# Layer 1's attention: the multiply by the reciprocal sums moved from chunk 1 to chunk 2, with a buffer of its own for the reciprocals

## The chip, the core and the metric

The kernel runs on one core of a Trainium2 chip. The core has a matrix engine (PE in the profile; its weight loads are listed apart as PEld), a vector engine (VectorE, DVE), a scalar engine (ScalarE, ACT), a general engine (GpSimd, POOL) and a queue engine that starts transfers (SyncE, SP). Each works through its own list of instructions; semaphores make one wait for another. Working memory is SBUF, and the matrix engine writes into PSUM. The metric is the device time of one execution in microseconds (us), the median of several runs.

## What is computed

Two layers, each a cross attention and a feed-forward network, over 8 batches of 112 tokens of width 512, with a context of 375 rows for each batch. The change lies in layer 1's attention. Cut to that part, the reference is:

```
q, k, v = proj(hs, Wq, bq), proj(at, Wk, bk), proj(at, Wv, bv)      # 16 heads of 32
scores = clip(einsum('bhsd,bhtd->bhst', q, k) / sqrt(32), -50, 50)
scores = clip(where(attend, scores, -10000.0), -50, 50)
probs  = softmax(scores, axis=-1)
ctx    = einsum('bhst,bhtd->bhsd', probs, v)                        # heads' outputs
delta  = rs * (ctx @ Wo.T + bo)
delta  = layernorm(delta) * gamma + beta
x      = x + delta
```

After it comes layer 1's feed-forward network with 8-bit weights, `down(silu(gate) * up)`, which takes the layer-normed x.

## The kernel before, in words

The softmax is taken without dividing first. For each batch the kernel forms e = exp(score), sums e times v into `num` and e alone into `den`, and multiplies `num` by the reciprocal of `den` at the end.

A loop runs over 8 batches b and, inside, over 3 chunks c of 125 context rows. In this stage the order on every engine is the order in which the program writes the instructions; it was laid out by hand. Each step (b, c) does:

- `scores(b, c)` (L894): 16 small matmuls (L900; 32 in the trace, two passes each) write the scores of the 16 heads into four PSUM tiles, one for each row group r. VectorE clips each of the four into an SBUF tile (L905), and ACT takes the exponential in place (L906). There are exactly four such PSUM tiles, so the scores of the next chunk can't begin before the clips of this one have read theirs.
- The SBUF tiles for e are three sets of four (`sets`). Chunk (b, c) uses set (b + c) modulo 3.
- `fill(1)`: one piece of the key and value projections of a later batch (L193 or L202) on the matrix engine. `STEPS` leaves it out in chunk 2 of batch 4.
- `sums` (L911): the matmuls of e with v (L926) for the chunk before. For the last chunk of a batch, which is summed in chunk 0 of the next batch, `den` too (L921). Its second operand is chunk 0's and 1's e added beforehand, `added`, by `add` (L892): on GpSimd for batches 0 to 6, on VectorE for batch 7. Then ACT copies `den` into `rden` (L932) and `num` into the columns b*112 to (b+1)*112 of `qT` (L933), where the queries of that batch were.
- Chunk 1: `divide(b - 1)` (L936) on VectorE: a reciprocal in place (L937) and a multiply of those columns of `qT` (L939).
- Chunk 2, from batch 2 on: `project_product(b - 2)`, the output projection of the tile of 128 tokens with that number. It reads columns (b-2)*128 to (b-1)*128 of `qT` (L798). `project_begin` (L804 and on) adds the bias and begins the layer norm on VectorE and GpSimd.
- Chunk 0, from batch 3 on: `project_end(b - 3)` (L817 and on) ends it and takes the moments of the next layer norm. `write4` and `transpose4` (L832, L839, L842, L843) prepare that tile for the feed-forward network; the transpose follows the projection on the matrix engine.

The weights of the feed-forward network are loaded and converted alongside (L864, L875, L877). After the loop the last batch is summed and divided, and the feed-forward network runs (L1026, L1044), beginning with two blocks of its gate and up products, then the last tile's projection.

Before the change, `rden` is `added[0]`: the first tile of the set that held the added e, free once the `den` matmuls have read it. The next to write it are the clips of chunk 2 of the following batch.

Of the kernel before, what the change touches and what calls it, by code (L numbers as in the profile page):

```python
# [23 lines left out]
F32 = mybir.dt.float32  # L24
# [11 lines left out]
P = 128  # L36
B, T, D = 8, 112, 512
KC = D // P
# [32 lines left out]
def two_layers(ctx: ExitStack, tc: tile.TileContext, x, ctxT, ctxN, mask0, mask1, w1, w2, w3,  # L71
# [10 lines left out]
    def slab(name, dtype=F32):  # L82
        return slabs.tile([P, SLAB], dtype, name=name, tag="slab")
# [126 lines left out]
    def fill(n=1):  # L210
        for _ in range(n):
            next(kv_steps, None)
# [602 lines left out]
    def project_end(i):  # L815
        d, f = updates.pop(i)
        nc.vector.scalar_tensor_tensor(xs[i], d, f, xs[i], ALU.mult, ALU.add)  # L817
        bn = stat.tile([P, nc.vector.BN_STATS_DIM], F32, name="bn", bufs=4)
        nc.vector.bn_stats(bn, xs[i])
        nc.vector.bn_aggr(mv4[:, i, :], bn)  # L820
        var = stat.tile([P, 1], F32, name="ln4_var")
        nc.vector.tensor_scalar_add(var, mv4[:, i, 1:2], LN_EPS)
        rsqrt_pool(var, rstd4[:, i:i + 1], "ln4")
# [22 lines left out]
    with tc.tile_pool(name="work2", bufs=1, side="right") as work2, \  # L846
            tc.tile_pool(name="ps_av", bufs=1, space=PSUM) as ps_av, \
            tc.manual_schedule(engines={ENGINES.PE, ENGINES.SP, ENGINES.DVE,
                                        ENGINES.Activation, ENGINES.Pool}):

        todo = [(w, which, half, c, min(PIECE, HALVES[which][half + 1] - c))
                for which, w in enumerate((wg, wu, wd)) for half in range(2)
                for c in range(HALVES[which][half], HALVES[which][half + 1], PIECE)]
        due = {(0, 1): 2, (0, 2): 2, (1, 0): 1, (1, 1): 2, (1, 2): 2, (2, 0): 1,
               (3, 1): 2, (3, 2): 2, (4, 0): 1, (5, 1): 2, (5, 2): 2, (6, 0): 1,
               (6, 1): 2, (6, 2): 2, (7, 0): 1, (7, 1): 2, (7, 2): 2}
        loaded = []

        def load_integers(count):
            for w, which, half, c, n in todo[:count]:
                raw = work2.tile([P, PIECE], I32, name="raw", bufs=2)[:, :n]
                nc.sync.dma_start(out=raw, in_=w[:, c:c + n])  # L864
                loaded.append((raw, which, half, c - HALVES[which][half], n))
            del todo[:count]

        def convert_integers():
            for raw, which, half, c, n in loaded:
                if (which, half) not in halves:  # L870
                    halves[which, half] = slab("w", F32R)
                t = halves[which, half][:, c:c + n]

                k = pieces.pop()
                nc.scalar.activation(t, raw, AF.Square, bias=zero_point,  # L875
                                     accum_out=squares[:, k:k + 1])
                nc.gpsimd.tensor_scalar(t, raw, -128.0, 1.0, ALU.add, ALU.mult)  # L877
            loaded.clear()

        sets = [[work2.tile([P, KC, T], F32, name=f"e{i}{r}") for r in range(NR)]
                for i in range(NCK)]

        def add(b):
            add = (nc.gpsimd if b in ADD_POOL else nc.vector).tensor_add
            for r in range(NR):  # L890
                e, e1 = (sets[(b + c) % NCK][r][:CK] for c in range(2))
                add(e, e, e1)  # L892

        def scores(b, c):  # L894
            kT = kvs_of[b][0]
            ss = [ps_s.tile([CK, KC, T], F32, name="s") for r in range(NR)]
            for dc in range(KC):
                for r in range(NR):
                    rows = slice(r * HD, (r + 1) * HD)
                    nc.tensor.matmul(ss[r][:, dc, :], lhsT=kT[rows, dc, c * CK:(c + 1) * CK],  # L900
                                     rhs=qT[rows, dc, b * T:(b + 1) * T], start=True, stop=True)
            es = sets[(b + c) % NCK]
            for r in range(NR):
                e = es[r][:CK]
                nc.vector.tensor_scalar(e, ss[r], upper[:, c, b:b + 1], -CLIP, ALU.min, ALU.max)  # L905
                nc.scalar.activation(e, e, AF.Exp, scale=SC1)  # L906
            return es

        def sums(b, c, es):  # L911
            if c == 0:
                sums.num = ps_av.tile([P, KC, T], F32, name="num")
            num = sums.num
            v = kvs_of[b][1]
            if c == NCK - 1:
                den = ps_av.tile([P, KC, T], F32, name="den")
                added = sets[b % NCK]
                for k, of in enumerate((added, es)):
                    for r in range(NR):  # L920
                        nc.tensor.matmul(den[r * HD:(r + 1) * HD], lhsT=ones[:CK, :HD],  # L921
                                         rhs=of[r][:CK], start=(k == 0), stop=(k == 1))
            for dc in range(KC):
                for r in range(NR):
                    head = slice((4 * dc + r) * HD, (4 * dc + r + 1) * HD)
                    nc.tensor.matmul(num[r * HD:(r + 1) * HD, dc, :], lhsT=v[:, c, head],  # L926
                                     rhs=es[r][:CK, dc, :], start=(c == 0 and dc == 0),
                                     stop=(c == NCK - 1 and dc == KC - 1))
            if c == NCK - 1:

                rden = added[0]
                nc.scalar.copy(rden, den)  # L932
                nc.scalar.copy(qT[:, :, b * T:(b + 1) * T], num)  # L933
                rdens[b] = rden

        def divide(b):  # L936
            nc.vector.reciprocal(rdens[b], rdens[b])  # L937
            cols = slice(b * T, (b + 1) * T)
            nc.vector.tensor_mul(qT[:, :, cols], qT[:, :, cols], rdens[b])  # L939


        STEPS = [3, 3, 3, 3, 2, 3, 3, 3]
        ADD_POOL = range(B - 1)
        last, rdens, later = None, {}, []
        counts = list(due.values())
        load_integers(counts.pop(0))
        for b in range(B):
            for c in range(NCK):
                if c == 2 and b in ADD_POOL:
                    add(b)  # L950
                if (b, c) in due:
                    convert_integers()
                    if counts:
                        load_integers(counts.pop(0))
                es = scores(b, c)
                if c == 2 and b not in ADD_POOL:
                    add(b)
                if c < STEPS[b]:
                    fill(1)
                if c == NCK - 1:  # L960
                    sums(*last)
                if (b, c) == (B - 1, NCK - 1):
                    over = tailp.tile([P, 29], F32, name="over")
                    nc.gpsimd.tensor_scalar(over, squares, WIDE, 1.0, ALU.is_gt, ALU.mult)
                if c == 0:
                    while later:
                        later.pop()()
                    if b >= 3:
                        project_end(b - 3)
                elif c == 1 and b >= 1:  # L970
                    divide(b - 1)
                elif c == 2:
                    turned = 3 <= b < 3 + GROUPS[0][1]
                    if turned:
                        write4(b - 3)
                    if b >= 2:
                        project_product(b - 2)
                    if b == B - 1:

                        hits = ps_s.tile([1, 29], F32, name="s")  # L980
                        nc.tensor.matmul(hits, lhsT=ones[:, :1], rhs=over, start=True, stop=True)
                        wide = tailp.tile([1, 1], I32, name="wide")
                        nc.vector.tensor_reduce(wide, hits, AX.X, ALU.max)
                    if b >= 2:
                        project_begin(b - 2)
                    if turned:
                        later.append(transpose4(b - 3, ps_mm, "mm"))
                if last and c < NCK - 1:
                    sums(*last)
                last = b, c, es  # L990

        nc.scalar.activation(stat.tile([CK, 1], F32, name="peak")[:], es[-1][:CK, 0, :1], AF.Silu)
        sums(*last)
        divide(B - 1)
        project_end(B - 3)
    kvs.close()

# [180 lines left out]
```

## Time and profile before

| | us |
|---|---|
| median of 3 runs | 523.79 (523.18 to 524.82) |
| the profiled execution | 523.3 |
| its span, first to last instruction | 521.4 |
| matmuls of scores, L900, whole kernel | 28.9 busy, 768 matmuls |
| clips, L905, whole kernel | 58.9 busy, 96 of 0.677 |
| reciprocals, L937, 8 of them | 2.94 each |
| multiplies, L939, 8 of them | 0.625 to 1.579, median 1.082 |
| add on GpSimd, L892, for one batch | 4.4 to 4.9 |

A row of an engine's timeline gives start, duration, engine, line, operation and tiles; "x4" means that four like instructions are merged into one row. A bracket at the end tells how long the engine stood idle before it, and what ended that. A row of the list of waits gives who waited for whom, the total, the number of times and the longest. Matmuls are pipelined: a group of them that lasts longer than its like has been held up inside, and the profile then counts the hold as busy.

### The profile page before, as it was taken

How to read it: one execution, taken by the hardware profiler on the slowest of the kernel's cores; microseconds unless marked ns; L12 is line 12 of the kernel's file. 1: busy time of each engine (PE TensorE's matmuls, PEld its weight loads, DVE VectorE, ACT ScalarE, POOL GpSimd, SP SyncE). 2: the span in 40 equal slices, each digit the busy share in tenths (PEclk: the TensorE clock that was granted, in tenths of full speed). 3: DMA queues.
4: the chain of work that ended last, by engine and by line, in shares of the span. 5: the costliest groups of instructions: out<-in, count | busy, mean ns of one | idle time of the engine just before them, and what ended most of it. 6: DMA issues, size and time to landing. Idle time of an engine off the chain costs nothing.

```text
span 521.4 us, 8802 instructions
## 1 busy us (share of the span) xinstructions
PE 504.7 (97%) x3380; PEld 317.0 (61%) x3380; DVE 335.7 (64%) x801; ACT 252.6 (48%) x438; POOL 134.8 (26%) x222
## 2 busy tenths in 40 slices
PE   9999999999999998889999999999999999999995
PEld 6445554454554455578655555555555788889983
DVE  3552548767788987784465588997897774434432
ACT  0336746857655656033876266466665224103310
POOL 0000211111011272020542376576762440000000
PEclk9999999999999999898999999999999999999998
DMA  8998795200210100041152111011321000010001
GB/s 232 334 411 345 252 350 189 70 2 0 87 54 1 60 2 0 2 143 52 52 170 64 60 49 44 23 51 38 86 63 52 22 1 1 16 46 20 1 20 45
DMA packets 13231, 45.75 MB, mean 88 GB/s; under 512 B 1969, under 2 KB 3008, under 8 KB 12032
## 3 DMA queue, kind: packets, MB, share of 16 engines
q1 hardware_dynamic: 11744, 41.43, 23.3%
q0 software_dynamic: 1280, 3.70, 2.1%
q8 instruction: 28, 0.46, 0.4%
q14 instruction: 19, 0.16, 0.1%
q10 hardware_dynamic: 160, 0.01, 0.0%
HBM read 41.46 MB, written 1.84 MB: 83 GB/s over the span
## 4 chain that ended last, share of the span: by engine, by line
PE 79%; DVE 12%; POOL 2%; ACT 2%; DMA 2%; issue 2%; DVEq 0%; ACTq 0%; POOLq 0%
PE mm L202 14%; PE s L1026 14%; PE mm L193 12%; PE down L1044 7%; PE mm L539 5%; PE mm L429 4%; PE mm L798 4%; PE s L400 4%; PE s L900 4%; PE num L926 3%; PE den L921 2%; PE mm L579 2%; DVE e L905 2%; DVE e L937 1%; DMA rs<-in_rscale_dram 1%
## 5 line engine op out<-in xcount | busy, mean ns | idle before, releaser
L202 PE MATMUL mm<-wv,cT 128*125 128x512 f32 x192 | 88.7, 606 | 0.0
L193 PE MATMUL mm<-cT,wk 128*128 128x375 f32 x256 | 87.4, 486 | 0.0
L1026 PE MATMUL s<-h4T,w 128*128 128x512 f32 (+1 forms) x352 | 72.6, 367 | 0.2 <-PE num L926 0.2
L905 DVE TENSOR_SCALAR e<-s,upper 125x448 f32<-125x448 f32 x96 | 58.9, 677 | 18.5 <-PE s L900 17.7
L1026 PEld LDWEIGHTS s<-h4T,w 128*128 128x128 f32 x352 | 63.6, 188 | 8.8 <-issue 0.5
L906 ACT ACTIVATE e<-e 125x448 f32<-125x448 f32 x96 | 51.8, 571 | 28.1 <-DVE e L905 27.5
L193 PEld LDWEIGHTS mm<-cT,wk 128*128 128x128 f32 x256 | 46.8, 190 | 27.6 <-issue 0.9
L202 PEld LDWEIGHTS mm<-wv,cT 128*125 128x125 f32 x192 | 35.0, 190 | 38.8 <-issue 37.2
L892 POOL TENSOR_TENSOR e<-e,e 125x448 f32<-125x448 f32 x28 | 33.3, 1221 | 14.6 <-PE num L926 14.6
L1044 PE MATMUL down<-w,gu 128*128 128x512 f32 x154 | 36.4, 393 | 0.0
L539 PE MATMUL mm<-w_q,q_qT 128*128 128x512 fp8e4 (+1 forms) x168 | 34.6, 361 | 1.6 <-ACT q_qT L351 1.1
L437 POOL DMA_DIRECT2D tokens<-x x14 | 10.7, 768 | 90.4 <-DVE x L431 62.7
L1034 ACT CAST gu<-gu 128x512 fp32r<-128x512 f32 (+1 forms) x22 | 12.5, 568 | 41.5 <-DVE gu L1032 41.5
L875 ACT ACTIVATE w<-raw,zero_point 128x640 fp32r<-128x640 int32 (+2 forms) x29 | 22.6, 782 | 20.1 <-DMA raw<-in_wd_dram 9.1
L1044 PEld LDWEIGHTS down<-w,gu 128*128 128x128 f32 x154 | 28.7, 188 | 6.1
L568 POOL TENSOR_SCALAR q<-gu 128x704 bf16<-128x704 f32 x14 | 10.8, 790 | 79.9 <-ACT gu L565 79.9
L877 POOL TENSOR_SCALAR w<-raw 128x640 fp32r<-128x640 int32 (+2 forms) x29 | 20.8, 727 | 38.7 <-DVE e L905 25.3
L900 PE MATMUL s<-qT,kv 32*125 32x112 f32 x768 | 28.9, 280 | 0.3
L539 PEld LDWEIGHTS <-q_qT 128*128 128x128 bf16 x168 | 16.3, 98 | 20.4 <-issue 1.9
L1032 DVE SCALAR_TENSOR_TENSOR gu<-s,su,gu 128x512 f32<-128x512 f32 (+1 forms) x22 | 15.0, 684 | 20.8 <-PE s L1026 19.2
L900 PEld LDWEIGHTS s<-qT,kv 32*125 32x125 f32 x768 | 24.2, 183 | 6.5 <-issue 4.9
L798 PE MATMUL mm<-wo,qT 128*128 128x512 f32 x56 | 25.8, 603 | 1.0 <-DVE qT L939 1.0
(237 smaller groups left out, 794.5 us busy)
## 6 DMA issues: line engine op xcount, KB each, us to landing
cT<-in_ctxT_dram SPq DMA_DIRECT2D x13, 750.0 KB, 6.0
raw<-in_w_dram SPq DMA_DIRECT2D x6, 1408.0 KB, 22.3
cN<-in_ctxN_dram SPq DMA_DIRECT2D x8, 768.0 KB, 5.7
raw<-in_wg_dram SPq DMA_DIRECT2D x8, 320.0 KB, 3.0
raw<-in_wu_dram SPq DMA_DIRECT2D x8, 320.0 KB, 2.9
raw<-in_wd_dram SPq DMA_DIRECT2D x8, 320.0 KB, 3.1
out_dram<-d SPq DMA_DIRECT2D x7, 256.0 KB, 2.0
wk<-in_wk_dram SPq DMA_DIRECT2D x4, 256.0 KB, 5.1
```

Source lines behind the costliest of these rows:

```text
L193: nc.tensor.matmul(ps[dc], lhsT=wk_s[:, kc, dc * P:(dc + 1) * P], rhs=cT[:, kc, :], start=(kc == 0), stop=(kc == KC - 1))
L202: nc.tensor.matmul(ps, lhsT=cT[:, kc, c * CK:(c + 1) * CK], rhs=wv_s[:, kc, :], start=(kc == 0), stop=(kc == KC - 1))
L400: nc.tensor.matmul(s, lhsT=hT0[b][:, kc, :], rhs=cTs[b][:, kc, :], start=(kc == 0), stop=False)
L539: nc.tensor.matmul(ps[:, :n], lhsT=qT[:, kc, :], rhs=w[:, kc * H + n0:kc * H + n0 + n], start=(kc == 0), stop=(kc == KC - 1))
L798: nc.tensor.matmul(ps, lhsT=qT[:, kc, i * P:(i + 1) * P], rhs=wo_s[:, kc, :], start=(kc == 0), stop=(kc == KC - 1))
L875: nc.scalar.activation(t, raw, AF.Square, bias=zero_point, accum_out=squares[:, k:k + 1])
L892: add(e, e, e1)
L900: nc.tensor.matmul(ss[r][:, dc, :], lhsT=kT[rows, dc, c * CK:(c + 1) * CK], rhs=qT[rows, dc, b * T:(b + 1) * T], start=True, stop=True)
L905: nc.vector.tensor_scalar(e, ss[r], upper[:, c, b:b + 1], -CLIP, ALU.min, ALU.max)
L906: nc.scalar.activation(e, e, AF.Exp, scale=SC1)
L1026: nc.tensor.matmul(ps[:, :n], lhsT=w[:, c:c + P], rhs=h4T[k][:, kc, :n], start=(kc == 0 and k == 0), stop=(kc == KC - 1 and k == 1))
L1044: nc.tensor.matmul(ps, lhsT=gus[k][:, hc, j * P:(j + 1) * P], rhs=w[:, c:c + D], start=(hc == 0 and k == 0), stop=(hc == HC - 1 and k == 1))
```

## The change

The reciprocals get a tile of their own in the stage's pool, `rden`, in place of `added[0]`. `divide` is split in two: `invert`, the reciprocal, stays in chunk 1; `scale`, the multiply, goes to chunk 2, behind that chunk's scores and clips (and in batch 7 behind the add on VectorE), ahead of `write4` and of the projection. After the loop both stand one after the other, as before.

```diff
-                rden = added[0]
+                rden = work2.tile([P, KC, T], F32, name="rden")
                 nc.scalar.copy(rden, den)
                 nc.scalar.copy(qT[:, :, b * T:(b + 1) * T], num)
                 rdens[b] = rden
 
-        def divide(b):
+        def invert(b):
             nc.vector.reciprocal(rdens[b], rdens[b])
+
+        def scale(b):
             cols = slice(b * T, (b + 1) * T)
             nc.vector.tensor_mul(qT[:, :, cols], qT[:, :, cols], rdens[b])
...
                 elif c == 1 and b >= 1:
-                    divide(b - 1)
+                    invert(b - 1)
                 elif c == 2:
+                    if b >= 1:
+                        scale(b - 1)
                     turned = 3 <= b < 3 + GROUPS[0][1]
                     if turned:
                         write4(b - 3)
...
         sums(*last)
-        divide(B - 1)
+        invert(B - 1)
+        scale(B - 1)
         project_end(B - 3)
```

## The prediction, made before the changed kernel was run

> **What bounds the kernel now.** I read the busy shares first, then what the matrix engine waited for, then its order of instructions beside VectorE's in the stage that the diff touches (the attention of layer 1, 244 to 403 us).
>
> ```profile
> PE 504.7 (97%) x3380; PEld 317.0 (61%) x3380; DVE 335.7 (64%) x801; ACT 252.6 (48%) x438; POOL 134.8 (26%) x222
> ...
> PE mm L798 <- DVE qT L939: 1.0, 1, 1.0
> ...
> 274.64 1.96 PE L900 MATMUL s<-qT,kv 32*125 32x112 f32 x32
> ...
> 308.31 1.79 PE L900 MATMUL s<-qT,kv 32*125 32x112 f32 x32
> ...
> 312.75 0.97 PE L926 MATMUL num<-e,kv 125*32 125x112 f32 x32
> 313.65 3.70 PE L798 MATMUL mm<-wo,qT 128*128 128x512 f32 x8
> ...
> 329.52 1.14 PE L900 MATMUL s<-qT,kv 32*125 32x112 f32 x32
> 330.60 0.97 PE L926 MATMUL num<-e,kv 125*32 125x112 f32 x32
> 332.56 3.70 PE L798 MATMUL mm<-wo,qT 128*128 128x512 f32 x8 [0.99 <-DVE qT L939]
> ...
> 308.84 2.94 DVE L937 RECIPROCAL e<-e 128x448 f32<-128x448 f32 x1
> 311.88 1.20 DVE L939 TENSOR_TENSOR qT<-qT,e 128x448 f32<-128x448 f32 x1
> 313.20 2.46 DVE L905 TENSOR_SCALAR e<-s,upper 125x448 f32<-125x448 f32 x4
> ...
> 328.84 2.94 DVE L937 RECIPROCAL e<-e 128x448 f32<-128x448 f32 x1
> 331.88 0.62 DVE L939 TENSOR_TENSOR qT<-qT,e 128x448 f32<-128x448 f32 x1
> 332.62 2.46 DVE L905 TENSOR_SCALAR e<-s,upper 125x448 f32<-125x448 f32 x4
> ```
>
> The matrix engine is busy 97% of the span. From here to the end nothing else sets the time for long, so each microsecond that it waits in this stage is a microsecond at the end, and a gain can only come from its waits. There are few. A group of score matmuls (L900) takes 1.14 us unhindered; at 274.64 it took 1.96 and at 308.31 it took 1.79, because its four PSUM tiles were still being clipped (L905): 0.82 and 0.65 us. A third at 369.00 took 1.48 (0.34). The projection (L798) waited 0.99 us for the multiply (L939) in batch 4, and a transpose waited 0.28 us for an ACT copy in batch 6. These five, 3.1 us, are the most that any faster order on VectorE could win here.
>
> The second thing to see is the order reciprocal (2.94 us), multiply (0.62 to 1.58 us), four clips (2.46 us), and how close the projection follows: in batch 3 the multiply ends at 313.08 and the projection starts at 313.65; in batch 4 it was already late.
>
> **What the Trainium skill says.** "TensorE: Matmul & The Clock Gate", section Architectural detail, says that VectorE takes its instructions strictly in order and that the matrix engine pulls only weight loads ahead, its matmuls staying in order. The trace agrees: every clip group and every L798 stands where the program puts it. "SBUF — State Buffer", section Who interferes with whom, says that a VectorE instruction with two SBUF inputs contends with a GpSimd instruction that reads SBUF. The trace agrees on the whole: the multiply took 0.63 us in batch 7 with GpSimd idle, and 1.20, 1.58 and 1.24 us beside GpSimd's adds (L892) in batches 3, 5 and 6. Of the clock gate the first page says (Part 1) that the array's clock halves after about one idle window of 3.4 us; no idle stretch of this stage is that long (granted clock 1.00 throughout), so nothing here shows it.
>
> **The change, part by part.**
>
> *The place.* The ACT copy of the sums (L932, 0.53 us) writes another buffer of the same shape; the reciprocal and multiply read it. No instruction is added. Its one buffer is rewritten in chunk 0 of the next batch, after the previous multiply, so nothing waits. In the tail ACT's first Silu (L1031) waits 4.65 us for L939, probably because its buffer lies over the old place; the matrix engine waits only 0.21 us around there, so releasing it is worth nothing. Cost 0.
>
> *The multiply behind the clips.* The clips of chunk 2 start about 1.1 us earlier (multiply 1.04 us, the mean of its eight, and two gaps). Who gains: the score matmuls of the next batch, if they wait on these clips. That is so once, at 274.64 (batch 2, chunk 0): its clips end at 275.43 and would end near 274.3, so 0.82 us goes. At 308.31 and 369.00 the matmuls wait for the clips of chunk 1, late through the layer norm of a previous tile, which the change doesn't move. From batch 2 on, the projection lies between chunk 2's clips and the next scores, so nothing is left to win.
>
> Who loses: project_product(b-2), in the same chunk 2, reads columns (b-2)*128 to (b-1)*128 of qT, and the multiply of batch b-1 writes (b-1)*112 to b*112. These overlap for every b from 2 to 7. So the projection still needs the multiply, which now stands behind four clips. With E the end of the reciprocal, the multiply is done at E + 2.46 + 1.04 = E + 3.5. The matrix engine's readiness is read from the trace. Its shift and VectorE's are the same from batch to batch, because VectorE's next work (L804) starts at the end of each projection.
>
> - b=2: E 289.11, done 292.6; projection ready 293.8. No wait, 1.2 us to spare.
> - b=3: E 311.78, done 315.28; ready 313.72. Wait 1.56.
> - b=4: E 331.78, done 335.28; it started at 332.56 before. 2.72 more than the old 0.99, 3.7 in all (scores and sums of this chunk have no key/value work between, STEPS[4] is 2).
> - b=5: E 350.56, done 354.06; ready 354.11. Nothing.
> - b=6: E 372.17, done 375.67; ready 374.11. Wait 1.56; the transpose's old wait of 0.28 behind it goes: 1.28.
> - b=7: here VectorE also does the add (L892, 2.23 us) between clips and multiply. E 392.38, done 398.11; ready 396.99. Wait 1.12, and VectorE now lags by the 0.28 that the matrix engine got back: 1.40.
> - b=8, after the loop: the same order as before, 0. project(6) finds the multiply done 2.9 us before it asks (408.11 against 410.97).
>
> Sum: -0.82 + 1.56 + 2.72 + 0 + 1.28 + 1.40 = +6.1 us. Behind the waiting projection stand the transpose and the next scores on the matrix engine, and L804 with a whole layer norm on VectorE and GpSimd; all move along, and after 403 us the matrix engine has no slack that would take a delay up.
>
> The profiled execution took 523.3 us (span 521.4 and 1.9 around it): 529.4. The median of the runs, 523.79, lies 0.49 above it: 529.9.
>
> **Bounds.** Unseen is what the multiply costs in its new position. All at 0.62: waits 1.14, 2.30, 0, 0.86 and 0.98, less 0.82: +4.5. All at 1.58: 2.10, 3.26, 0.49, 1.82 and 1.94, less 0.82: +8.8. I take the mean of the eight, since GpSimd's adds and conversions reach over the new position in batches 3, 5 and 6, and are nearly over in batch 4. So 528.3 to 532.6 for this mechanism. The wait in batch 4 is near the clock window's length; one such window at half speed would be an estimate of 1.7 us from that page, and below nothing it can't go.
>
> **The rivals.**
>
> 1. As forecast: the multiply becomes the last to arrive at the projection. For it: the dependency by columns and the traced times. 529.9, chance 0.72.
>
> 2. The other side, not slower: the multiply stays hidden, and only the earlier clips count. Place: the score groups of the next batch, price 0.82 us, up to the five waits' 3.1 us if the earlier clips also speed the exponentials and PSUM copies behind them. It decides from the point where the projection gets ready later than E + 3.5 us (E + 5.7 in batch 7). For it: batches 2 and 5 meet this, the latter by 0.05 us. Against: batches 3, 4, 6 and 7 miss it by 1.1 us or more. 523.0, at best 520.7; chance 0.09, of which 0.05 within what counts as no change.
>
> 3. Only part of it bites: VectorE gets through its chain sooner than I add up, and only batches 4 and 7 wait: -0.8 + 2.3 + 1.0 = +2.5, 526.3. For it: batches 3 and 6 depend on when GpSimd's port comes free. Against: even the fast multiply leaves about 1 us there. Chance 0.08.
>
> 4. More: every multiply slow (+8.8), and a clock window lost (1.7): 532.6 to 534.3. For it: GpSimd's busy stretches and the long gap of batch 4. Chance 0.09.
>
> 5. The change doesn't do what it says, the multiply landing where it was: 523.8. Against: VectorE's order is the program's. Chance 0.02.
>
> **How the numbers follow.** The measurement tells about 0.3% (1.6 us) from no change. Slower: rivals 1, 3 and 4, 0.89. No change: 0.05 of rival 2 and rival 5, 0.07. Faster: the rest of rival 2, 0.04. The range is 1's bounds, drawn down to take in half or more of rival 3 and up a little into rival 4: 526.6 to 532.9.
>
> **What would show it.** In the new profile: L798 waiting for the multiply four times, some 1.6, 3.7, 1.6 and 1.4 us in batches 3, 4, 6 and 7, none in 2; no score group of 1.96 us in batch 2, chunk 0; clips starting directly after each reciprocal; VectorE's busy time the same within 3 us (only the port's share of the multiply can change); the stage from 403 us on as long as before, only later. I am wrong if L798 doesn't wait on VectorE, or if waits appear in the tail instead.

## The result, and the profile after

The changed kernel takes 531.37 us (median of 4 runs, 530.74 to 532.34) where the kernel before takes 523.54 in the same comparison: a ratio of 1.0147, 95% interval 1.0123 to 1.017, 7.8 us slower. The profiled execution has a span of 529.6 us against 521.4; of that difference of 8.2 us, 8.1 lie between batch 1's first scores and the feed-forward network (152.30 us against 144.21; called the stage below).

The busy shares, the list of what the matrix engine waited for, and the rows of its output projection (L798) and of VectorE's reciprocal, clips and multiply (now L941) answer to the lines shown of the kernel before:

```profile
PE 505.2 (95%) x3380; PEld 316.4 (60%) x3380; DVE 337.0 (64%) x801; ACT 252.3 (48%) x438; POOL 132.8 (25%) x222
```

```profile
PE mm L798 <- DVE qT L941: 6.5, 3, 3.1
...
PE mm L798 <- ACT w L875: 2.2, 2, 1.7
```

```profile
274.13 1.14 PE L900 MATMUL s<-qT,kv 32*125 32x112 f32 x32
...
292.44 3.70 PE L798 MATMUL mm<-wo,qT 128*128 128x512 f32 x8
...
314.06 3.67 PE L798 MATMUL mm<-wo,qT 128*128 128x512 f32 x8 [1.69 <-DVE qT L941]
...
335.06 5.25 PE L798 MATMUL mm<-wo,qT 128*128 128x512 f32 x8 [3.10 <-DVE qT L941]
...
358.62 3.67 PE L798 MATMUL mm<-wo,qT 128*128 128x512 f32 x8 [0.47 <-ACT w L875]
...
380.36 3.67 PE L798 MATMUL mm<-wo,qT 128*128 128x512 f32 x8 [1.72 <-ACT w L875]
...
404.50 3.70 PE L798 MATMUL mm<-wo,qT 128*128 128x512 f32 x8 [1.72 <-DVE qT L941]
```

```profile
307.49 2.94 DVE L937 RECIPROCAL rden<-rden 128x448 f32<-128x448 f32 x1
310.35 2.36 DVE L905 TENSOR_SCALAR e<-s,upper 125x448 f32<-125x448 f32 x4
312.63 1.29 DVE L941 TENSOR_TENSOR qT<-qT,rden 128x448 f32<-128x448 f32 x1
...
334.34 0.66 DVE L941 TENSOR_TENSOR qT<-qT,rden 128x448 f32<-128x448 f32 x1
...
400.84 3.05 DVE L892 TENSOR_TENSOR e<-e,e 125x448 f32<-125x448 f32 x4
403.82 0.62 DVE L941 TENSOR_TENSOR qT<-qT,rden 128x448 f32<-128x448 f32 x1
```

Three things are to be seen. The busy times are the same as before within 2 us; what was added is waiting. The projection waits in five of its six calls in the loop, and each time starts just after the multiply's end: 312.63 + 1.29 is 313.92, and it starts at 314.06; in batch 4, 334.34 + 0.66 is 335.00, and it starts at 335.06. (Two of the waits are put down to ACT's conversion L875, which ended a little later than the multiply; an experiment below shows that they are the multiply's.) And in batch 4 the projection itself lasts 5.25 us, not 3.70. The granted clock in short stretches there (start and end, length, then busy time by engine; the third number from the end is the clock of the matrix engine) tells why:

```profile
329.00:332.00 3.00, 2.95 (x97) 2.43 (x96) 3.00 (x2) 1.35 (x3) 2.21 (x4) 1.00 0.03 5
332.00:335.00 3.00, 0.00 (x0) 0.00 (x0) 3.00 (x7) 2.28 (x4) 2.52 (x3) 0.96 0.01 3
335.00:337.00 2.00, 1.94 (x3) 0.91 (x4) 0.46 (x2) 0.03 (x1) 0.00 (x0) 0.50 0.00 0
337.00:339.00 2.00, 2.00 (x5) 0.94 (x4) 0.00 (x0) 0.00 (x0) 0.00 (x0) 0.70 0.00 0
```

While the matrix engine idled for 3.1 us its clock fell to half, and it stayed there for about 3.2 us of the projection (0.50 over two, and 0.70 over the next two). Half of that, 1.6 us, is what the projection lost: 5.25 against 3.70.

The starts of the projections, after minus before, give the account. They are -1.33, +0.41, +2.50, +4.58, +6.32 and +7.58 us for batches 2 to 7, and +7.58 for the feed-forward network. Read as differences:

| Place | forecast, us | measured, us |
|---|---|---|
| before batch 1's sums | 0 | -0.51 |
| scores of batch 2, chunk 0 (1.96 to 1.14) | -0.82 | -0.82 |
| wait, batch 3 | +1.56 | +1.74 |
| wait, batch 4 (beyond the old 0.99) | +2.72 | +2.09 |
| batch 4's projection at half clock | 0 | +1.54 |
| wait, batch 5 | 0 | +0.54 |
| wait, batch 6, less the transpose's old wait | +1.28 | +1.24 |
| wait, batch 7 | +1.40 | +1.79 |
| feed-forward network | 0 | +0.62 |
| sum | +6.1 | +8.2 |

The first and the last measured rows lie in parts that the change doesn't touch: differences between two executions. The part from the feed-forward network on took 118.2 to 119.1 us over all the profiles of this study, with no order by kernel.

### The profile page after: what moved, and what is told of

The parts are those of the page before. It is cut to its first block, busy times and chain, and to the rows that moved or that the text cites. A ratio compares the mean times of both kernels' runs of the same rounds, so it can differ in the third digit from the quotient of the medians.

```text
span 529.6 us, 8788 instructions
## 1 busy us (share of the span) xinstructions
PE 505.2 (95%) x3380; PEld 316.4 (60%) x3380; DVE 337.0 (64%) x801; ACT 252.3 (48%) x438; POOL 132.8 (25%) x222
## 4 chain that ended last, share of the span: by engine, by line
PE 73%; DVE 14%; DMA 3%; POOL 3%; ACT 3%; issue 2%; SPq 0%; ACTq 0%; POOLq 0%; DVEq 0%
PE s L1031 14%; PE mm L193 12%; PE mm L202 11%; PE down L1049 7%; PE mm L798 5%; PE mm L539 5%; PE mm L429 4%; PE s L400 4%; PE s L900 2%; DVE e L905 2%; PE num L926 2%; PE mm L579 2%; DVE rden L937 2%; PE den L921 2%; DMA rs<-in_rscale_dram 1%
## 5 line engine op out<-in xcount | busy, mean ns | idle before, releaser
L905 DVE TENSOR_SCALAR e<-s,upper 125x448 f32<-125x448 f32 x96 | 58.5, 671 | 17.5 <-PE s L900 17.5
L798 PE MATMUL mm<-wo,qT 128*128 128x512 f32 x56 | 27.3, 632 | 8.7 <-DVE qT L941 6.5
L892 POOL TENSOR_TENSOR e<-e,e 125x448 f32<-125x448 f32 x28 | 30.9, 1137 | 13.9 <-PE num L926 13.9
L875 ACT ACTIVATE w<-raw,zero_point 128x640 fp32r<-128x640 int32 (+2 forms) x29 | 22.6, 780 | 22.1 <-DMA raw<-in_wd_dram 9.4
```

The lines of the kernel that those rows point to most:

```text
L798: nc.tensor.matmul(ps, lhsT=qT[:, kc, i * P:(i + 1) * P], rhs=wo_s[:, kc, :], start=(kc == 0), stop=(kc == KC - 1))
L875: nc.scalar.activation(t, raw, AF.Square, bias=zero_point, accum_out=squares[:, k:k + 1])
```

## The experiments

The theory: the projection reads columns of `qT` that the multiply writes, so it waits for whatever stands before the multiply on VectorE; the wait is the loss, and where it is long the clock can fall too. Rivals: the new buffer costs something, VectorE is late for other work, or the slow projection has a cause of its own. Times are to be read against the kernel before on the same chip: its median was 524.68 us beside the place alone, the dependency taken away, batch 4 alone and the work in batch 4's gap; 522.97 beside batch 1 alone, the add moved and the split; 523.85 beside the repeat, the first try in all four gaps and the split with `write4` ahead; 523.45 beside the second try and GpSimd taken out. Differences in us are differences of these medians, unless a ratio is said. The stage's time is that of the profiled execution.

**The place alone.** The multiply is moved back to chunk 1; `rden` stays in its own tile.

```diff
+        LATE = ()
...
                     invert(b - 1)
+                    if b not in LATE:
+                        scale(b - 1)
                 elif c == 2:
-                    if b >= 1:
+                    if b in LATE:
                         scale(b - 1)
```

> The reciprocals' own tile alone; the multiply stays in chunk 1. Theory (the projection waits for the late multiply): 0 against the kernel before, 523.2 to 523.9 us, the score group in chunk 0 of batch 2 stalls again by 0.8 us, the projection of batch 4 waits 1.0 us. Rival (the new place costs or gives something, through waits on its single buffer or the room below it): a difference of over 1 us.

Measured: 524.48 us, ratio 0.9999 (0.9983 to 1.0015). In the trace the score group of batch 2 took 1.76 us again and batch 4's projection waited 0.97 us. The place is worth nothing that can be told (within 0.9 us), and the rival falls.

**The dependency taken away.**

```diff
-            nc.vector.tensor_mul(qT[:, :, cols], qT[:, :, cols], rdens[b])
+            divided = work2.tile([P, KC, T], F32, name="divided")
+            nc.vector.tensor_mul(divided, qT[:, :, cols], rdens[b])
```

> The changed kernel, with every multiply of chunk 2 written to a tile of its own, so that the projection reads the heads' outputs undivided: the division is left out of what is computed, all instructions remain. Theory (the whole loss is the projection waiting for the multiply, with its clock): the waits in batches 3, 4, 6 and 7 vanish, the gain of 0.8 us in batch 2 stays, and the wait of 1.0 in batch 4 goes too: 521.5 to 523 us. Rival (VectorE is late for the next batch's work, or the port is fought over, whatever the projection waits for): 526 us or more.

Measured: 522.67 us, ratio 0.9958 (0.9946 to 0.997), 2.0 us below before (2.2 by the ratio). The projections of batches 3 to 6 in its trace:

```profile
314.31 3.70 PE L798 MATMUL mm<-wo,qT 128*128 128x512 f32 x8
332.15 3.70 PE L798 MATMUL mm<-wo,qT 128*128 128x512 f32 x8
353.85 3.70 PE L798 MATMUL mm<-wo,qT 128*128 128x512 f32 x8
373.85 3.70 PE L798 MATMUL mm<-wo,qT 128*128 128x512 f32 x8
```

No row has a wait. VectorE still runs every multiply in its late place, and ACT every conversion, so the waits put down to ACT were the multiply's. This settles the cause: without the dependency the whole loss goes, and the old wait of batch 4 with it. The gain of the earlier clips stays: the score group of batch 2 took 1.14 us.

**One batch alone: 4.** The multiply is late only there: the edit of the place alone, with `LATE = (4,)`.

> Only batch 4's multiply goes behind the clips. Theory with the clock (an idle stretch of 3.1 us makes the projection behind it take 5.2 us, not 3.7): +2.1 for the wait and +1.5 for the clock, +3.6 us, so 527.1. Without the clock, the long projection of the changed kernel being something else of its own: +2.1 us, 525.6.

Measured: 527.19 us, ratio 1.0065 (1.0043 to 1.0087), so +2.3 to +4.6 us. In the profiled execution the wait is the same, the projection longer still:

```profile
335.62 6.45 PE L798 MATMUL mm<-wo,qT 128*128 128x512 f32 x8 [3.11 <-DVE qT L941]
```

The ten runs lie in two bunches, six from 526.4 to 527.2 us and four from 528.9 to 530.3; the profiled one is 529.24. The mean granted clock was 0.985 in each of the four and 0.990 or 0.991 in each of the six. So it looks as if the wait is fixed and the clock's part is not: the six have a median of 526.7, +2.0, where +2.1 had been forecast without the clock. No profile was kept of one of the six. Over all ten, +2.1 is just below the interval.

**One batch alone: 1.** The same edit, with `LATE = (1,)`.

> Only batch 1's multiply goes behind the clips, where no projection follows. Theory (the one score group that waits on chunk 2's clips gets them earlier): -0.8 us, 522.7. Rival (the gain is taken back further on, the next thing being late anyway): 523.5, no change.

Measured: 522.43 us, ratio 0.9984 (0.9969 to 0.9998), or -0.8 us by the ratio and -0.5 by the medians, at the edge of what can be told. The trace shows the score group at 1.14 us, and the stage took 143.52 us against 144.21.

**Work in the gap of batch 4.** Three matmuls into a PSUM tile that nobody reads.

```diff
+                    if b == 4:
+                        extra = ps_mm.tile([P, D], F32, name="mm")
+                        for _ in range(3):
+                            nc.tensor.matmul(extra, lhsT=ones, rhs=wo_s[:, 0, :],
+                                             start=True, stop=True)
                     if b >= 2:
                         project_product(b - 2)
```

> The changed kernel, with three matmuls into an unread PSUM tile ahead of batch 4's projection, about 2.7 us of the 3.1 that the matrix engine idles there. Theory (the clock fell in the idle stretch): the projection takes 3.7 us again and the time falls by 1.5 us against the changed kernel, to +6.5 against before. Rival (the slow projection is something else, for instance its operands): no change, +8, or more if the extra matmuls delay it.

Measured: 529.79 us, ratio 1.0097 (1.0071 to 1.0123), +5.1 us where +6.5 had been expected. Batches 4 and 7 in its trace:

```profile
336.06 3.67 PE L798 MATMUL mm<-wo,qT 128*128 128x512 f32 x8 [0.43 <-ACT e L906]
...
404.08 5.40 PE L798 MATMUL mm<-wo,qT 128*128 128x512 f32 x8 [1.88 <-DVE qT L941]
```

With the gap filled, batch 4's projection runs at full clock, as expected. But in this profiled execution (532.18 us, the slowest of the four) the clock fell in batch 7 instead, behind a gap of only 1.88 us.

**Work in all four gaps, first try.** The same with one, three, one and one matmuls in batches 3, 4, 6 and 7, beside a repeat of the changed kernel.

> The changed kernel once more, beside the next two on one chip. Theory: +8 us against the kernel before, as the first time; the projection behind the idle stretch of 3.1 us in batch 4 runs at half clock for a part again, the ones behind stretches of 1.7 us may or may not.

> The changed kernel, with matmuls into an unread PSUM tile ahead of the projections of batches 3, 4, 6 and 7 (one, three, one and one, 0.9 us each), so that no idle stretch stays over 1 us. Theory (waits for the multiply and, on top, the clock lost in idle stretches): every projection takes 3.7 us; the waits stay as they were, so -1.5 us against the changed kernel, +6.5 against before. Rival (the extra matmuls only fill, and the clock plays no part): +8 as without them.

The repeat gave 531.6 us, ratio 1.0149 (1.0132 to 1.0165), with waits of 1.68, 3.10, 0.48, 1.72 and 1.75 us and a slow projection of 5.40 us in batch 4: the same picture. The filled kernel was a miss: 536.16 us, ratio 1.0236 (1.0201 to 1.0272). Batches 3 and 6 show why:

```profile
315.99 3.70 PE L798 MATMUL mm<-wo,qT 128*128 128x512 f32 x8 [2.10 <-ACT kv L196]
...
382.98 5.40 PE L798 MATMUL mm<-wo,qT 128*128 128x512 f32 x8 [2.78 <-ACT kv L196]
```

There are two `mm` tiles. With the extra one between the key/value piece and the projection, the projection had to have the piece's tile back, and ACT copies that out only behind this chunk's exponentials. In batch 4, where no piece comes before, it had worked.

**Work in all four gaps, second try.**

```diff
+        EXTRA = {3: 1, 4: 3, 6: 1, 7: 1}
...
+                    if b in EXTRA:
+                        extra = ps_av.tile([P, KC, T], F32, name="den")
+                        for _ in range(EXTRA[b]):
+                            nc.tensor.matmul(extra, lhsT=ones, rhs=wo_s[:, 0, :KC * T].rearrange("p (k t) -> p k t", t=T),
+                                             start=True, stop=True)
```

> The changed kernel, with matmuls ahead of the projections of batches 3, 4, 6 and 7 (one, three, one and one, 0.8 us each) into the PSUM tile of the sums of e, which is free in chunk 2: the earlier kernel with such matmuls took a tile that ACT still had to copy out, and waited for that. Theory (waits plus clock): every projection takes 3.7 us, the waits themselves stay, -1.5 us against the changed kernel, +6.5 against before. Rival (the clock plays no part): +8.

Measured: 529.68 us, ratio 1.0121 (1.0094 to 1.0149), +6.2 us. Every projection of the loop took 3.67 or 3.70 us. The stage took 149.96 us against 152.30 in the changed kernel: about 1.5 of the 2.3 us is the clock, and 0.8 the add of batch 7, which took 2.22 us here and not 3.05. In time the two kernels' intervals (1.0094 to 1.0149, and 1.0123 to 1.017 for the changed one) overlap, so it is the trace that carries this.

**The add behind the multiply in batch 7.**

```diff
                 if c == 2 and b not in ADD_POOL:
+                    scale(b - 1)
                     add(b)
...
-                    if b >= 1:
+                    if b >= 1 and b in ADD_POOL:
                         scale(b - 1)
```

> The changed kernel, with batch 7's multiply between its clips and the add on VectorE, no longer behind the add. Theory (clips, add and multiply stand one after the other in front of the projection): the wait of 1.7 us in batch 7 goes, -1.7 us against the changed kernel, +6.3 against before. Rival (the projection then waits for something else, or the later add holds up the sums of the last chunk): less than 0.5 us gained.

Measured: 529.55 us, ratio 1.0122 (1.0087 to 1.0156), +6.6 us. The projection of batch 7 no longer waits, and the stage is 1.6 us shorter than in the changed kernel:

```profile
402.86 3.70 PE L798 MATMUL mm<-wo,qT 128*128 128x512 f32 x8
```

**GpSimd taken out.**

```diff
-                nc.gpsimd.tensor_scalar(t, raw, -128.0, 1.0, ALU.add, ALU.mult)
...
-                if c == 2 and b in ADD_POOL:
-                    add(b)
```

> The changed kernel, leaving out GpSimd's adds of e in batches 0 to 6 and its half of the weights' conversion, so that the sums and weights are not those of the reference; GpSimd then reads no SBUF beside the multiplies. Theory (the multiply and batch 7's add are stretched by GpSimd's reads): every multiply in the loop takes 0.62 us, the add 2.2 us, the waits in batches 3, 6 and 7 shrink by 0.65, 0.65 and 0.8 us and that of 0.5 in batch 5 goes; -2.6 us against the changed kernel, +5.4 against before. Rival (the multiply is slow for another reason, or the wait is set by ACT's conversions): less than 0.5 us gained.

Measured: 527.86 us, ratio 1.0082 (1.0062 to 1.0102), +4.4 us where +5.4 had been expected. Batches 3 to 7 (the multiply is L940 and ACT's exponential L905 here):

```profile
314.91 3.67 PE L798 MATMUL mm<-wo,qT 128*128 128x512 f32 x8 [1.01 <-ACT e L905]
335.73 3.70 PE L798 MATMUL mm<-wo,qT 128*128 128x512 f32 x8 [2.92 <-DVE qT L940]
357.20 3.70 PE L798 MATMUL mm<-wo,qT 128*128 128x512 f32 x8
378.13 3.67 PE L798 MATMUL mm<-wo,qT 128*128 128x512 f32 x8 [1.01 <-ACT e L905]
401.22 3.70 PE L798 MATMUL mm<-wo,qT 128*128 128x512 f32 x8 [0.67 <-DVE qT L940]
```

The multiplies of the loop took 0.61 to 0.62 us, and the waits fell by 0.68, 0.18, 0.47, 0.71 and 1.05 us, 3.1 in all where 2.6 had been expected. The stage took 147.53 us against 152.30 in the changed kernel: 3.1 of the 4.8 us are these waits, and 1.5 the clock, which in this execution did not fall behind a gap of 2.92 us.

**A version that could beat both: the divide split by columns.** What the projection of this chunk reads is divided in chunk 1, the rest behind the clips.

```diff
-        def invert(b):
-            nc.vector.reciprocal(rdens[b], rdens[b])
-
-        def scale(b):
-            cols = slice(b * T, (b + 1) * T)
-            nc.vector.tensor_mul(qT[:, :, cols], qT[:, :, cols], rdens[b])
+        def divide(b, t0, t1):
+            part = rdens[b][:, :, t0:t1]
+            nc.vector.reciprocal(part, part)
+            cols = slice(b * T + t0, b * T + t1)
+            nc.vector.tensor_mul(qT[:, :, cols], qT[:, :, cols], part)
+
+        def needed(b):
+            return (b - 1) * P - (b - 1) * T if b >= 2 else 0
...
-                    invert(b - 1)
+                    if needed(b):
+                        divide(b - 1, 0, needed(b))
                 elif c == 2:
                     if b >= 1:
-                        scale(b - 1)
+                        divide(b - 1, needed(b), T)
...
-        invert(B - 1)
-        scale(B - 1)
+        divide(B - 1, 0, T)
```

> Each reciprocal and multiply is split by columns: those that the next projection reads, 16*(b-1) of 112, are divided in chunk 1, the rest behind chunk 2's clips (all of them in batch 1). Theory (only the part that the projection reads is urgent): the 0.8 us of batch 2 and the 1.0 us of batch 4 both go, nothing waits anew: -1.8 us, 521.7. Rival (the late part pushes the layer norm on VectorE behind it, or the extra instructions cost as much): 523.5 or more.

Measured: 522.74 us, ratio 0.9993 (0.9982 to 1.0003), no change where -1.8 us had been expected. Both waits went, but a new one came: the transpose behind batch 4's projection waited for `write4`, which the late part now held up.

```profile
335.17 0.63 PE L839 MATMUL mm<-ident,d 128*128 128x128 f32 x4 [0.97 <-DVE d L832]
```

**The same, with `write4` ahead of the late part.** The edit is to the split kernel.

```diff
-                    if b >= 1:
-                        divide(b - 1, needed(b), T)
                     turned = 3 <= b < 3 + GROUPS[0][1]
                     if turned:
                         write4(b - 3)
+                    if b >= 1:
+                        divide(b - 1, needed(b), T)
```

> The split kernel, with write4 ahead of the late part of the divide. Theory (in the split kernel the late part pushed write4, and so the transpose behind the projection of batch 4, by 1.0 us): that wait goes, the stage takes 1.8 us less than in the kernel before, 521.2 to 522 where before has 523.0 to 523.8. Rival (what is late next is the layer norm's first step behind the late part, and takes it back): 0.7 us less at most, as the split kernel.

Measured: 523.2 us, ratio 0.999 (0.998 to 1.0001). The transpose's wait in batch 4 went, and the next thing late was L804, as the rival had it: it reads the projection out of its PSUM tile, and a key/value piece wanted that tile.

```profile
336.58 3.70 PE L202 MATMUL mm<-wv,cT 128*125 128x512 f32 x8 [0.63 <-DVE d L804]
```

The stage is 1.1 us shorter than before in the trace, 143.13 against 144.21; in time it can't be told from no change.

## Why the prediction was right

- *The dependency by columns, and the direction.* Right, and shown: with the dependency taken away the waits and the whole loss go.
- *The place costs nothing.* Right (0.9999).
- *The gain of 0.82 us, once, in batch 2.* Right, in the changed kernel and with batch 1's multiply alone moved.
- *The waits.* Forecast +6.14 with the gain, measured +6.6 without the clock (1.74 + 2.09 + 0.54 + 1.24 + 1.79 - 0.82). The places are right, and the sum comes so near in part by luck, since errors of size cancel in it. The multiply in its new place was put at 1.04 us; it took 1.29, 0.66, 1.56, 1.32 and 0.62 us in batches 3 to 7. The four clips ahead of it were put at 2.46 us; in batches 3 to 6 the multiply starts 2.19 to 2.34 us after the reciprocal's end. The 0.06 to 0.15 us between the multiply's end and the projection's start were not counted. In batches 3 and 6 the first two errors nearly cancel. In batch 4 they add up, and the wait is 0.63 us shorter than forecast. Batch 5's wait comes from its slow multiply.
- *Batch 7.* Here the add took 3.05 us and not 2.23, and the fast multiply hides it: the multiply ends 5.79 us after the reciprocal's end, where 5.73 was forecast. The loss is larger mainly because the transpose's old wait in batch 6 was worth more than the 0.28 us of the list: from the projection's start to the next scores it was 4.57 us, and it is 4.04 now.
- *What the multiply costs.* With GpSimd out of the way the multiplies take 0.61 to 0.62 us, so GpSimd's instructions make the difference. That it is their reads is what the Trainium skill says ("SBUF — State Buffer", section Who interferes with whom); no run here parts reads from writes. The mean of the old places was wrong for each single new one; a multiply lying under GpSimd's adds should have been priced at 1.2 to 1.58 from the rows of batches 3, 5 and 6.
- *The clock.* The step that failed. I left it at 0 in the sum, because no idle stretch seen was as long as the 3.4 us that the Trainium skill ("TensorE: Matmul & The Clock Gate", Part 1) gives, though my own sum made batch 4's gap 3.7; I put it into rival 4 only, at 1.7 us. It cost 1.54 us: the stage is 8.1 us longer with it, and without it 6.6 would stand against the forecast of 6.1. The measurements differ from the page's figure (last section).
- *The tail.* Silu's wait of 4.65 us, which I put down to the old place of `rden`, stayed with the new one: 4.6 us on the multiply again. That it costs nothing was right; why it is there isn't settled.

## What to carry to other kernels

Before a step is moved behind others on an in-order engine, list who reads its result in the same stretch, and race the two chains from their last common point: in this kernel the end of one projection, to the start of the next. Here four of six batches lost more than a microsecond each, for a gain of 0.82 us in one place. Moving part of the work helps only if what then stands behind that part has slack; each time one wait was taken away here, the next reader in line (a transpose, then a PSUM tile) took its turn. A gap on the matrix engine can cost more than its length: that of 3.10 us here cost 1.54 more.

## What the hardware showed that I had not expected

The matrix engine's clock fell to half behind idle stretches that I had thought too short for it. In this stage it fell behind stretches of 3.10 us (the changed kernel, its repeat, and the one with the add moved), 3.11 (batch 4 alone), 2.78 and once 1.88 us; it didn't behind one of 2.92 and one of 2.10, nor behind any of 1.75 or less. The projection behind it then took 5.25 to 6.45 us in place of 3.70. From the clock's mean in the stretches of idle time, taking one fall to one half, it came about 2.8 us after the last matmul in the changed kernel (0.96 over 3 us) and about 1.8 us after it with batch 4 alone (0.76 over 2.6 us).

So the gap's length alone doesn't decide. The traces show what fits better. Read in steps of 0.25 us, the half clock lasts from 334.8 to 338.2 us in the changed kernel, from 404.2 to 407.6 in the one with work in batch 4's gap, and from 334.4 to 341.2 with batch 4 alone: 3.41 us, 3.41, and twice that. The stretches at full clock between two falls are whole multiples of 3.41 us too (119.5 us, 35 of them, before the changed kernel's fall).

Laid out in windows of this length, counted from those edges, the matrix engine was idle for 54% to 83% of the window just before each of the six falls in this stage, and for 50% at most of any other full-clock window there, over all 14 profiles. The gap of 2.92 us lay across two windows, idle for 50% and 36% of them. So what counts in these traces is whether more than about half of one window is idle. That depends on where in the windows a gap lies, and this differs between executions: the fall came 0.27 us before batch 4's projection started in the changed kernel, and 1.16 us after it in the repeat.

The cost follows as well, as half of what is left of the half-clock stretch once work resumes: (3.41 - 0.27) / 2, 1.6 us, in the changed kernel (measured 1.55); 3.41 / 2, 1.7 us, in the repeat (1.70); (6.83 - 1.26) / 2, 2.8 us, with batch 4 alone (2.75). All this is read from the traces; no run set the place of a gap in the windows. Outside this stage the line is less sharp: in the kernel before, the clock fell at 234.5 us after a window that was idle for 49%.
